# Layer 1 and the exponentials of the first four samples at other places in a planner's order

## The chip, the cores and the metric

The kernel runs on one core of a Trainium2 chip. The metric is the device time of one execution in microseconds (us). The core's engines work side by side, each through its own queue in a fixed order: TensorE (PE) for matrix products, VectorE (DVE), ScalarE (ACT), GpSimd (POOL), and SyncE (SP), which here only issues transfers. Sixteen DMA engines carry the transfers.

## What is computed

Sixteen samples of 64 x 64 tokens with 256 channels pass through four layers; each normalizes its input by groups of eight channels and adds its result. Cut to what matters:

```python
x = x + L0(_gn(x), embeddings)   # nearest of 1024 codes per token
x = x + L1(_gn(x), Wf, bf, Wg, bg, Wh, bh)
x = x + L2(_gn(x), w1, b1, w2, b2, w3, b3)
x = x + L3(_gn(x), w_qkv, w_out, b_out, gamma, beta)

# L0: indices = argmin(|x|^2 + |e|^2 - 2 x e); quantized = e[indices]
# L1: f, g, h = x Wf + bf, x Wg + bg, x Wh + bh
#     out = sigmoid(f g^T) h            (per image row of 64 tokens)
# L2: x0, x1, x2 = x.w1 + b1, x.w2 + b2, x.w3 + b3     (n = 4096 tokens)
#     sm = softmax(x0[:, :, None] * x1[:, None, :], axis=1)
#     gate = sigmoid(einsum('bn,bnm->bm', x2, sm)); out = gate * x
# L3: linear attention with 4 heads, an output projection, a layer norm
```

Layer 2 is the heavy one for DVE and ACT: for each sample 4096 x 4096 exponentials, each multiplied and summed.

## The kernel before

Each sample passes through a row of tasks, each a Python generator that emits some instructions, then yields the number of planner steps that they stand for:

- `stats0`: loads the sample in eight chunks of 512 tokens and takes the statistics of the first normalization.
- "search" (`stage1`, layer 0): 32 tiles of 128 tokens. For each, eight matmuls against the 1024 codes (L403), a DVE pass that adds and finds the largest score (L409), one that finds its index (L414), and a gather of the code's row by POOL (L415). Per chunk the result is turned round on PE (L378), its statistics are taken (L266) and it is stored.
- "layer1" (`layer1`): loads the weights, scales them by the statistics, then for eight chunks: load (L453), the projections (L482, L493), the scores (L513), their activation, and one chunk later the mixing matmuls (L533), the addition (L538), statistics (L266) and the store (L545).
- "rows" (`rows2`): reads the eight chunks again (L590), forms the three rows of layer 2 (L593), writes them to memory and reads them back spread over all partitions (`spread_rows`, L615: 1 MB for each of two rows and halves).
- "exps" (`stage2`): 64 pairs of one ACT exponential (L645, 128 x 2048) and one DVE multiply and sum (L648); at the end the gate, stored.
- "gate" (`gate2`): loads each chunk and its gates (L693, L695), ACT forms the factor (L702), DVE applies it (L703) and takes statistics, and the chunk is stored (L709).
- "layer3" (`stage3`): two passes over the chunks and the output.

Samples overlap. Times in the plan are in periods; the search of sample b has the period from b to b + 1. For every other task the planner (L946 to L958) names a time from which it may start, here `end + LAG...` after the task before it, and a length. `task` (L940) moves a start back to the end of the same kind of task of the sample before, so that exponentials of two samples never overlap in the plan, nor two layers 1. In the end a heap (L961 to L968) draws the steps of all tasks in the order of planned time: a step of s out of `total` moves its task on by `length * s / total`. The order in which the steps are drawn is the order of precedence of their instructions; the framework arranges each engine's queue by it, though an instruction that is ready may be placed before one of higher precedence that is not. Some short chains stand under `tc.high_priority` and go ahead of others.

The constants: `LAG1` 0.06 and `LEN1` 0.7 for layer 1 (0.2 long for sample 0, 0.35 for the last), `LAGR` 0.03 and 0.1 for rows, `LAG2` 0.17 from the end of layer 1 to the exponentials and 1.0 for these, `LAG3` 0.06 and `LENG` 0.8 for the gate, `LAG4` 0.04 and 1.0 for layer 3. Shorter lengths hold at the end of the batch (`LEN3`, 0.65, 0.15). The statistics of samples 1 to 7 are planned in the first 1.58 periods (`FILL`).

By this arithmetic layer 1 of samples 0, 1, 2 stands at 1.06-1.26, 2.06-2.76, 3.06-3.76; rows at 1.29-1.39, 2.79-2.89, 3.79-3.89; exponentials at 1.43-2.43, 2.93-3.93, 3.93-4.93; gates at 2.49-3.29, 3.99-4.79, 4.99-5.79; layer 3 at 3.33-4.33, 4.83-5.83, 5.83-6.83. From sample 1 on each is one period after that of the sample before.

Buffers that tie the tasks together: two wide PSUM tiles shared by L403, L493 and L533; two each of `x0b` and `x2b`, the spread rows; three of `ex`; four of `xb`, shared by the loads of stats0, rows and layer 3; three of `xm` for layer 1.

Of the kernel before, what the change touches and what calls it, by code (L numbers as in the profile page):

```python
# [32 lines left out]
LAG1, LEN1 = 0.06, 0.7  # L33
LAGR = 0.03
LAG2 = 0.17
LAG3, LENG = 0.06, 0.8
LAG4 = 0.04
LEN3 = {0: 0.4, 1: 0.33, 2: 0.37}
FILL = ((0.05, 0.95, 2), (1.0, 1.27, 3), (1.4, 1.58, 2))
EARLY = sum(n for _, _, n in FILL)  # L40


@with_exitstack
def kernel(
# [25 lines left out]
    def bank(name):  # L70
        return ps_m.tile([P, 512], F32, tag="pm", name=name)
# [60 lines left out]
    def busy(t, n):  # L132

        for _ in range(n):
            nc.tensor.matmul(
                t[:, :512], lhsT=ones3, rhs=ones3.unsqueeze(1).to_broadcast([P, 4, P]), start=True, stop=True,
                skip_group_check=True,
            )
# [174 lines left out]
    def stats0(b):  # L313
        tag = f"s0_{b}"
        st = stats_tile(0, f"st_{tag}")
        src = xT[b].rearrange("(k p) n -> p k n", p=P)
        for ch in range(NCHUNK):
            xt = xb.tile([P, NK, CW], F32, tag="xb", name=f"xs_{tag}_{ch}")
            nc.sync.dma_start(out=xt, in_=src[:, :, ch * CW : (ch + 1) * CW])
            chunk_stats(st, xt, ch)  # L320
            yield 1.5
        with tc.high_priority(offset=URGENT):
            norm0[b] = gn_finish(st, "n0", b)
        yield 2
# [242 lines left out]
    def rows2(b):  # L567
        tag = f"r2_{b}"
        scale, nmean, _ = norm2[b]
        with tc.high_priority(offset=URGENT):  # L570
            pb = bank(f"pbr_{tag}")
            busy(pb, 3)
            for k in range(NK):
                nc.scalar.activation(
                    wrow_n[:, k, :].rearrange("p (j n) -> p j n", n=32)[:, :, 0:3],
                    wrow_raw[:, k : k + 1, 0:3].to_broadcast([P, 4, 3]), AF.Copy, scale=scale[:, k : k + 1],
                )
            for k in range(NK):
                nc.tensor.matmul(
                    pb[:, 0:1], lhsT=wrow_n[:, k, :], rhs=nmean[:, k : k + 1], start=(k == 0), stop=(k == NK - 1)  # L580
                )
            brow_n = small.tile([P, 1], F32, tag="brow_n", name=f"brow_{tag}")
            nc.scalar.activation(brow_n, pb[:, 0:1], AF.Identity, bias=brow)
        x01 = small.tile([P, NT, 2], F32, tag="x01", name=f"x01_{tag}", bufs=2)
        rd = dram.tile([3, 2, 4, CW], F32, tag="rows", name=f"rows_{tag}", bufs=3)
        for h in range(2):
            pr = bank(f"pr_{tag}_{h}")
            for j in range(4):
                xt = xb.tile([P, NK, CW], F32, tag="xb", name=f"xr_{tag}_{h}_{j}")
                nc.sync.dma_start(out=xt, in_=x2_d[b][4 * h + j])  # L590
                part = slice(32 * j, 32 * j + 32)
                for k in range(NK):
                    nc.tensor.matmul(  # L593
                        pr[part, :], lhsT=wrow_n[:, k, part], rhs=xt[:, k, :], start=(k == 0), stop=(k == NK - 1)
                    )
            rows = s1p.tile([P, CW], F32, tag="t4", name=f"rows_{tag}_{h}", bufs=3)
            nc.scalar.activation(rows, pr, AF.Identity, bias=brow_n)
            for n in range(3):
                nc.scalar.dma_start(out=rd[n, h], in_=rows[n : n + 97 : 32, :])
            pt = bank(f"prt_{tag}_{h}")  # L600
            for t in range(CH):
                nc.tensor.transpose(pt[:, t * P : (t + 1) * P], rows[:, t * P : (t + 1) * P], ident)
            nc.vector.tensor_copy(
                x01[:, 16 * h : 16 * h + 16, :].rearrange("p (j t) n -> p j t n", t=CH),
                pt.rearrange("p (t j n) -> p j t n", j=4, n=32)[:, :, :, 0:2],
            )
            yield 4
        rows_d[b] = x01, rd, [spread_rows(rd, b, 0)]

    def spread_rows(rd, b, h):  # L610

        x0b = s2p.tile([P, TOK // 2], F32, tag="x0b", name=f"x0b_{b}_{h}", bufs=2)
        x2b = s2p.tile([P, TOK // 2], F32, tag="x2b", name=f"x2b_{b}_{h}", bufs=2)
        for dst, n in ((x0b, 0), (x2b, 2)):
            nc.sync.dma_start(  # L615
                out=dst, in_=rd[n : n + 1, h, :, :].rearrange("o j n -> o (j n)").to_broadcast([P, TOK // 2])
            )
        return x0b, x2b
# [314 lines left out]
    b = 0  # L933
    for begin, end, n in FILL:
        for k in range(n):
# [4 lines left out]
    def task(stage, ready, length, gen, total):  # L940
        start = max(ready, free.get(stage, 0.0))
        free[stage] = start + length
        tasks.append((start, length, gen, total))
        return start + length

    for b in range(nb):  # L946
        left = nb - 1 - b
        if b > EARLY:
            tasks.append((b - 0.7, 0.5, stats0(b), 14))
        task("search", b, 1.0, stage1(b), 160)  # L950
        end = task("layer1", b + 1 + LAG1, (LEN1 if b else 0.2) if left else 0.35, layer1(b), 88)
        task("rows", end + LAGR, 0.1, rows2(b), 8)
        if left:
            end = task("exps", end + LAG2, 1.0, stage2(b), 160)
            end = task("gate", end + LAG3, 0.15 if left == 1 else LENG, gate2(b), 36)
        else:
            end = task("exps", end + LAG2, 0.65, stage2(b, NCHUNK), 200)
        task("layer3", end + LAG4, LEN3.get(left, 1.0), stage3(b), 160)  # L958
    for _ in stats0(0):
# [45 lines left out]
```

## Time and profile before

| what | value |
|---|---|
| runs | 5691.64, 5671.38, 5691.11 us, median 5691.11 |
| profiled execution | 5674.06 us, span 5672.1 us, mean granted clock of TensorE 0.962 |
| exponentials (L648, DVE) | 1024, busy 2360.4 us, 2312 ns each |
| exponentials (L645, ACT) | 1024, busy 2138.6 us, 2089 ns each |
| score matmuls (L403, PE) | 4096, busy 1971.1 us |
| score and index (L409, L414, DVE) | busy 619.9 and 622.9 us |
| from HBM and to it | 751.18 MB and 303.04 MB, 186 GB/s over the span |

In the trace the searches (first to last L403) of samples 0 to 5 run from 31 to 175, 176 to 471, 473 to 724, 726 to 1021, 1021 to 1327 and 1334 to 1649 us; later ones take 320 to 338 us, and the last ends at 4973 us. The exponentials on ACT (L645) of samples 0 to 3 start at 322, 712, 1012 and 1309 us, and those of sample 0 end at 584. The last exponential of sample 15 starts at 5505 us.

Busy time of an engine is the union of its instructions' spans. Matmuls overlap each other in a pipeline and their ends are modelled, so a busy PE is not a PE at its peak. A view of stretches gives each engine's busy time between two moments, with the mean clock that the throttle granted to TensorE and the share of the DMA engines in use.

### The profile page before, as it was taken

The numbers are of one execution on the slowest core, as the hardware profiler recorded it, in microseconds if no ns is written. First come the engines' busy times: TensorE is split into PE (matmuls) and PEld (weight loads), VectorE is DVE, ScalarE is ACT, GpSimd is POOL, SyncE is SP. The second block draws the span as 40 slices with busy tenths as digits, with TensorE's granted clock in tenths as the row PEclk, the third lists the DMA queues.
The fourth block names the chain that finished last, engine by engine and source line by source line (L and its number), as shares of the span: only waits on it lengthen the run. The fifth ranks groups of instructions, "written<-read, shape, count | busy, mean of one in ns | idle before, by whom it ended". The sixth has DMA issues, their size and how long they took to land.

```text
span 5672.1 us, 76096 instructions
## 1 busy us (share of the span) xinstructions
PE 5162.0 (91%) x26927; PEld 3189.6 (56%) x26927; DVE 5049.3 (89%) x7186; ACT 4571.1 (81%) x6642; POOL 1801.5 (32%) x1076
## 2 busy tenths in 40 slices
PE   7977889989999999999999999999999999987788
PEld 3534446545656566565655656565565656564556
DVE  7589799899999999999999999999999999988882
ACT  4468589888989898888978888898888879887873
POOL 2223234323333333334333333333333333321221
PEclk9988999999999999999999999999999999998889
DMA  8553744655665757566575656657575675745543
GB/s 254 174 178 84 232 115 144 214 163 185 196 198 175 224 159 236 171 211 198 185 234 155 216 185 200 210 173 236 160 224 183 201 219 156 222 149 176 200 157 119
DMA packets 521365, 1059.26 MB, mean 187 GB/s; under 512 B 52504, under 2 KB 266392, under 8 KB 512792
## 3 DMA queue, kind: packets, MB, share of 16 engines
q1 hardware_dynamic: 406288, 885.11, 46.5%
q0 software_dynamic: 73728, 67.14, 8.3%
q10 hardware_dynamic: 40968, 102.13, 4.6%
q8 instruction: 214, 3.51, 0.3%
q14 instruction: 167, 1.37, 0.1%
HBM read 751.18 MB, written 303.04 MB: 186 GB/s over the span
## 4 chain that ended last, share of the span: by engine, by line
PE 46%; DVE 17%; ACT 16%; issue 6%; DMA 5%; POOL 4%; SPq 0%; ACTq 0%; DVEq 0%; POOLq 0%
PE pd_s L403 14%; ACT ex_s L645 7%; DVE ex_s L648 7%; PE ph_l L493 4%; PE pxo_s L908 3%; PE pqv_s L782 3%; PE po_l L533 2%; PE pk_s L765 2%; ACT nn_s L398 2%; POOL qv_s L802 2%; PE pz_s L857 2%; DVE i_s L414 2%; DVE nn_s L409 2%; PE pxo_s L902 2%; PE pvr_s L865 2%
## 5 line engine op out<-in xcount | busy, mean ns | idle before, releaser
L648 DVE CUSTOM_DVE_ANT_0 ex_s<-ex_s,x2b 128x2048 f32<-128x2048 f32 x1024 | 2360.4, 2312 | 77.6 <-ACT ex_s L645 74.6
L645 ACT ACTIVATE ex_s<-x0b,nmax_s,x_r 128x2048 f32<-128x2048 f32 x1024 | 2138.6, 2089 | 40.7 <-DVE num_s L648 30.5
L403 PE MATMUL pd_s<-e,xn_s 128*128 128x512 f32 x4096 | 1971.1, 614 | 43.9 <-DVE m L409 27.9
L415 POOL DMA_INDIRECT xc_s<-in_emb_rows,i_s x512 | 1113.7, 2175 | 1852.7 <-DVE i_s L414 1337.5
L403 PEld LDWEIGHTS pd_s<-e,xn_s 128*128 128x128 f32 x4096 | 745.8, 195 | 778.8 <-issue 669.1
L409 DVE CUSTOM_DVE_ANT_0 nn_s<-pd_s,nn_s 128x1024 f32<-128x1024 f32 x512 | 619.9, 1212 | 113.5 <-PE pd_s L403 63.0
L414 DVE FIND_INDEX8 i_s<-m,nn_s 128x8 uint32<-128x1024 f32 x512 | 622.9, 1217 | 0.0
L398 ACT ACTIVATE nn_s<-ne,nx_s 128x1024 f32<-128x1024 f32 x512 | 582.5, 1143 | 33.1 <-DVE nx_s L369 18.7
L493 PE MATMUL ph_l<-wh_l,xt_l 128*128 128x256 f32 x2048 | 519.6, 390 | 28.7 <-DVE m L409 16.9
L782 PE MATMUL pqv_s<-wqv_s,xk_s 128*128 128x256 f32 x2048 | 489.3, 381 | 0.0
L493 PEld LDWEIGHTS ph_l<-wh_l,xt_l 128*128 128x128 f32 x2048 | 379.7, 192 | 138.9 <-issue 69.0
L782 PEld LDWEIGHTS pqv_s<-wqv_s,xk_s 128*128 128x128 f32 x2048 | 389.1, 191 | 120.6 <-issue 59.7
L802 POOL TENSOR_TENSOR qv_s<-qv_s,qm_s 128x512 f32<-128x512 f32 x128 | 221.6, 1731 | 662.6 <-DVE qm_s L801 363.2
L868 POOL TENSOR_TENSOR lrs_s<-lrs_s,mhalf 128x4 f32<-128x4 f32 x128 | 178.0, 1391 | 677.2 <-ACT lrs_s L867 663.3
L756 POOL TENSOR_TENSOR qv_s<-qv_s,qd_s 128x512 f32<-128x512 f32 x128 | 214.4, 1675 | 249.0 <-DVE qd_s L755 132.0
L533 PE MATMUL po_l<-blk,h_l 128*128 128x128 f32 x2048 | 282.1, 288 | 3.0 <-DVE m L409 1.5
L533 PEld LDWEIGHTS po_l<-blk,h_l 128*128 128x128 f32 x2048 | 260.6, 200 | 41.1 <-issue 24.5
L908 PE MATMUL pxo_s<-wctx_s,qo_s 128*128 128x256 f32 x1024 | 269.2, 386 | 2.2 <-DVE qo_s L876 2.2
L765 PE MATMUL pk_s<-xk_s,wk_s 128*128 128x512 f32 x512 | 256.0, 620 | 1.0 <-DMA xk_s<-x_g 0.9
L913 ACT COPY y_s<-pxo_s 128x512 f32<-128x512 f32 x256 | 147.5, 580 | 132.4 <-PE pxo_s L912 116.0
L378 PE MATMUL pt_s<-ident,xc_s 128*128 128x128 f32 x1024 | 156.7, 282 | 105.2 <-DMA xc_s<-in_emb_rows,i_s 79.0
L351 ACT ACTIVATE sq_s<-xt_s,first 128x512 f32<-128x512 f32 x256 | 200.2, 806 | 37.2 <-DMA x0b<-rows_r 21.0
(206 smaller groups left out, 7322.0 us busy)
## 6 DMA issues: line engine op xcount, KB each, us to landing
xs_s<-in_xT SPq DMA_DIRECT2D x128, 512.0 KB
xt_s<-in_xT SPq DMA_DIRECT2D x128, 512.0 KB
xc_s<-in_x SPq DMA_DIRECT2D x128, 512.0 KB
x_s<-xt_s ACTq DMA_DIRECT2D x128, 512.0 KB
xt_l<-x_s SPq DMA_DIRECT2D x128, 512.0 KB
x_l<-xt_l SPq DMA_DIRECT2D x128, 512.0 KB
xr_r<-x_l SPq DMA_DIRECT2D x128, 512.0 KB
xg_g<-x_l SPq DMA_DIRECT2D x128, 512.0 KB
```

Of the source, the lines that this page charges most:

```text
L398: nc.scalar.activation(nn, ne2, AF.Identity, bias=nx2[ch][:, t : t + 1])
L403: nc.tensor.matmul(pd[:, cols], lhsT=xn[ch][:, k, t * P : (t + 1) * P], rhs=e2[:, k, cols], start=(k == 0), stop=(k == NK - 1),)
L409: nc.vector.tensor_tensor_reduce(out=nn, in0=pd, in1=nn, scale=1.0, scalar=-3.0e38, op0=ALU.add, op1=ALU.max, accum_out=m8[:, 0:1],)
L414: nc.vector.max_index(i8, m8, nn)
L415: nc.gpsimd.indirect_dma_start(out=xc[ch][:, t, :], out_offset=None, in_=emb_rows, in_offset=bass.IndirectOffsetOnAxis(ap=i8[:, 0:1], axis=0),
L493: nc.tensor.matmul(ph[:, t, :], lhsT=X[:, k, t * P : (t + 1) * P], rhs=wh_n[:, k, :], start=(t % 2 == 0 and k == 0), stop=False, skip_grou ...
L533: nc.tensor.matmul(po[:, m : m + P], lhsT=h[:, t, k * P : (k + 1) * P], rhs=at[:, t, :, :].rearrange("p r i -> p (r i)"), start=True, stop ...
L645: nc.scalar.activation(ex, x0b, AF.Exp, bias=nmax[:, T : T + 1], scale=x01[:, T, 1:2], accum_out=den[:, h, T : T + 1])
L648: nc.vector.tensor_tensor_reduce(out=ex, in0=ex, in1=x2b, scale=1.0, scalar=0.0, op0=ALU.mult, op1=ALU.add, accum_out=num[:, h, T : T + 1],)
L765: nc.tensor.matmul(pk, lhsT=wk_n[:, k, :], rhs=xt[:, k, :], start=(k == 0), stop=(k == NK - 1))
L782: nc.tensor.matmul(pqv[:, j, :], lhsT=xt[:, k, t * P : (t + 1) * P], rhs=wqv_n[:, k, :], start=(j == 0 and k == 0), stop=False, skip_group ...
L908: nc.tensor.matmul(px[:, j, :], lhsT=qT[:, t * P : (t + 1) * P], rhs=wctx[:, 1, :], start=False, stop=False, skip_group_check=True,)
```

## The change

A table `RAMP` gives samples 0 to 3 five numbers of their own: the lag of layer 1 after the search, its length, the length of rows, the lag from layer 1's end to the exponentials, and the length of these. Other samples keep the old constants.

```diff
 EARLY = sum(n for _, _, n in FILL)
+RAMP = {0: (0.03, 0.15, 0.05, 0.13, 1.25), 1: (0.04, 0.3, 0.06, 0.14, 1.2), 2: (0.05, 0.45, 0.08, 0.16, 1.14), 3: (0.06, 0.58, 0.1, 0.17, 1.08)}
...
         task("search", b, 1.0, stage1(b), 160)
-        end = task("layer1", b + 1 + LAG1, (LEN1 if b else 0.2) if left else 0.35, layer1(b), 88)
-        task("rows", end + LAGR, 0.1, rows2(b), 8)
+        early, len1, lenr, early2, lenx = RAMP.get(b, (LAG1, LEN1, 0.1, LAG2, 1.0))
+        end = task("layer1", b + 1 + early, len1 if left else 0.35, layer1(b), 88)
+        task("rows", end + LAGR, lenr, rows2(b), 8)
         if left:
-            end = task("exps", end + LAG2, 1.0, stage2(b), 160)
+            end = task("exps", end + early2, lenx, stage2(b), 160)
             end = task("gate", end + LAG3, 0.15 if left == 1 else LENG, gate2(b), 36)
```

By the same arithmetic layer 1 of samples 0 to 3 then stands at 1.03-1.18, 2.04-2.34, 3.05-3.50 and 4.06-4.64, rows at 1.21-1.26, 2.37-2.43, 3.53-3.61 and 4.67-4.77, and exponentials at 1.31-2.56, 2.56-3.76, 3.76-4.90 and 4.90-5.98. The exponentials of sample 4 start at 5.98 in place of 5.93, since those of sample 3 end there, and each later sample keeps this 0.05; gates and layer 3 follow the exponentials. Searches, the statistics ahead of them, and layer 1 and rows from sample 4 on stay where they were. No instruction and no transfer is added or taken away.

## The prediction

> **What bounds the kernel now.** I read the head of the page first, then the span cut into stretches at the places where the exponentials of a sample begin or end, then the groups of single lines. A "period" is the planner's unit: one search of a sample.
>
> ```profile
> span 5672.1 us, 76096 instructions
> PE 5162.0 (91%) x26927; PEld 3189.6 (56%) x26927; DVE 5049.3 (89%) x7186; ACT 4571.1 (81%) x6642; POOL 1801.5 (32%) x1076
> ...
> PE   7977889989999999999999999999999999987788
> ...
> DVE  7589799899999999999999999999999999988882
> ACT  4468589888989898888978888898888879887873
> ```
>
> The middle of the span is full; what is missing from VectorE (DVE) lies in the first eight slices and the last six. The DVE and ScalarE (ACT) work is the same in any order, so the sum below is made in idle DVE time. The stretches (columns: length, busy us of PE, PEld, DVE, ACT, POOL with counts, granted clock, DMA share, GB/s):
>
> ```profile
> 180.00:322.00 142.00, 135.32 (x836) 82.01 (x837) 67.95 (x117) 62.24 (x121) 23.37 (x25) 0.96 0.55 176
> 322.00:589.00 267.00, 193.23 (x778) 97.11 (x777) 254.34 (x327) 215.59 (x259) 82.70 (x39) 0.87 0.40 116
> 589.00:717.00 128.00, 113.93 (x558) 59.62 (x557) 85.61 (x149) 66.64 (x104) 29.52 (x22) 0.97 0.80 254
> 717.00:1012.00 295.00, 275.16 (x1405) 161.46 (x1404) 270.17 (x374) 259.42 (x368) 102.89 (x55) 0.96 0.46 140
> 1012.00:1309.00 297.00, 267.43 (x1392) 157.35 (x1392) 280.82 (x374) 258.94 (x352) 89.57 (x48) 0.95 0.61 191
> 1309.00:1628.00 319.00, 308.03 (x1671) 192.28 (x1670) 303.42 (x428) 283.10 (x412) 113.33 (x64) 1.00 0.62 193
> ```
>
> The first row is layer 1 of sample 0 beside the search of sample 1: PE busy 135 of 142, DVE 68. The second is exponentials of sample 0, the third the pause before those of sample 1: DVE idles 128 - 85.6 = 42.4 us. The last row is an ordinary period: 15.6 of 319 idle, 4.9%. That the third row is a pause of this kind, the line of the ACT exponentials shows, restricted to 570 to 730 us:
>
> ```profile
> L645 ACT ACTIVATE ex_s<-x0b,nmax_s,x_r x11: 2079/2088/2105, 568.4 to 729.1; 128x2048 f32<-128x2048 f32 x11
> ```
>
> Eleven in 160 us, none between 584 and 712 (the pieces of the timeline), against one every 5 us in an ordinary period (64 in 319). They are missing because sample 1's rows come last: the row matmuls (L593) run from 685 to 702, and the exponentials wait for them. And the plan's times are only an order of precedence, not a clock:
>
> ```profile
> L702 ACT ACTIVATE u_g<-gb_g,one,gn_s_n x16: 797/804/835, 604.3 to 658.4; 128x512 f32<-128x512 f32 x16
> ```
>
> These are all 16 gate activations of sample 0: planned over 0.8 of a period, they ran in 54 us of the pause. Sample 4's, in the same view, are spread over 195 us (1976 to 2171). Idle slots are already filled with later work where it is ready.
>
> **The change, part by part.** No instruction is added or removed, and no DMA or its size changes. What moves is worked out from the planner's arithmetic. Layer 1 of samples 0 to 3 goes from 1.06-1.26, 2.06-2.76, 3.06-3.76, 4.06-4.76 to 1.03-1.18, 2.04-2.34, 3.05-3.50, 4.06-4.64; exponentials from 1.43-2.43, 2.93-3.93, 3.93-4.93, 4.93-5.93 to 1.31-2.56, 2.56-3.76, 3.76-4.90, 4.90-5.98. Gates and layer 3 follow them; from sample 4 on every exponential, gate and layer 3 is 0.05 period later against searches, layer 1 and rows, which stay.
>
> (1) The pause. The exponentials of sample 1 follow those of sample 0 directly, since its rows now end at 2.43 instead of 2.89. If that stretch gets an ordinary period's idle share, DVE gains 42.4 - 0.049 x 128 = 36 us. This is the main term.
>
> (2) The earlier start of sample 0, 1.31 for 1.43. What it no longer waits for is 0.12 x 32 = 3.8 search tiles, each 8 matmuls of L403 that stood at 3.43 us in the chain of waits: 13 us. In the first row DVE idles 74 of 142, 52%; 13 us of that are 7 us. The lower bound is nothing, if the chain from layer 1's end (rows, their store, the 1 MB broadcast) sets it; I take 7.
>
> (3) The change from sample 1 to sample 2. From 717 to 1012 DVE idles 24.8 against 0.049 x 295 = 14.5 expected; the last exponential of sample 1 ends on ACT at 989, sample 2's first starts at 1012, because its row matmuls end at 999. Rows now end 0.15 period ahead of the exponentials instead of 0.04. I take 8 of the 10.3; the other two I leave to search.
>
> (4) What crowding costs. Layer 1 of sample 0 ran between 199 and 287, 88 us, beside 0.2 x 32 = 6.4 tiles of 3.43, 22 us: 66 us of PE time for layer 1. In the new 0.3 period of sample 1 PE has 66 + 9.6 tiles x 3.43 = 99 us. DVE has there 9.6 x (1.21 + 1.22) for L409 and L414, 15.4 exponentials (0.3/1.25 of 64) x 2.31, and layer 1's 8 x (1.21 + 2 x 0.68) for L538 and L266: 23 + 36 + 21 = 80. So PE sets the pace and DVE may idle 19 us. For sample 2 (0.45) the same sum is PE 66 + 49 = 115 against DVE 35 + 55 + 21 + 11 of gate = 122: nothing. For sample 3 layer 3 of sample 0 lies beside it and PE is ahead again; the nearest row is sample 1's, so 19 more at most. Bounds 0 to 38; I take 12, because sample 0's gate shows that idle slots take later work, and exponentials of the same sample are ready there.
>
> (5) The end. After the search's end (4973 us in the trace, 16.0 in the plan) 0.05 period more is left: 0.05 x 64 = 3.2 exponentials x 2.31 = 7.4 us, and 0.05/0.8 of a gate's 24 us, 1.5. As DVE work it is missing ahead of 4973, where it would have run at 95% busy; in the tail it runs at 86% (220.4 of 253 and 246.9 of 290 busy): 9/0.86 - 9/0.95 = 1 us. If the tail is set by its own chain, all 9 count. I take 5.
>
> (6) The middle, samples 4 to 13, has the same work in each period and I cost it at nothing. What hides the shift is that the change from one sample's exponentials to the next (ACT has none for 9.8 us, 2611.1 to 2620.9) is covered by search tiles. Rival B takes that cover away.
>
> (7) DMA and queues. SP's queue gets layer 1's loads and stores (16 of 512 KB per sample) in a denser order, and rows' eight loads in 0.05 to 0.1 period. From 640 to 717 the DMA share is 0.82, and layer 1 of sample 1 with its wide traffic now moves to about 500 to 589, where it is 0.35. SP's longest waits in the ramp are behind L342, for the gather (24.1 us); behind it wait only loads one or two chunks ahead. Bounds -5 to +10, taken as 0.
>
> (8) The clock. From 340 to 500 PE is busy 100.6 of 160 and its granted clock is 0.82; two more stretches without layer 1 arise (about 2.43-3.05 and 3.61-4.06). With DVE at 153.6 of 160 there, slower PE costs nothing; without that cover it is 18% of 100 us, 18 us, a bound.
> The Trainium skill's "TensorE: Matmul & The Clock Gate", section "HAM oscillation — how this bites in real kernels", speaks against the change: PE gaps over some 3.4 us drop the clock to half, so a burst after each gap starts slow. By the row the sum is left as it is; by the rule, with the 18 us paid once, it would halve to a gain of 16.
>
> Sum: -36 - 7 - 8 + 12 + 5 = -34 us. The profiled execution took 5674.06 us (span 5672.1 and 2 around it): 5640. Its runs were 5671 to 5692 with median 5691.11, 17 above the profiled one; the same 34 from the median give 5657, which I forecast.
>
> **Rivals.** A: the pause is filled and all is given back. For: the local sums of (4) reach 38, the tail 9; 36 + 7 + 8 - 38 - 9 = 4 us gained: 5687. Against: exponentials are ready during layer 1's bursts, so DVE has something to take.
>
> B, slower: the 0.05 period costs in each later period. 0.05 x 333 us (1952 to 2285) is 17 us: the change of exponentials (2611 to 2621) moves to about 2628 to 2638, right against the change of search, where PE goes from its last tile to the next sample's first (2638 to 2645; DMA share 0.97 just ahead). With neither search tiles nor exponentials DVE has only layer 3. Place: eleven changes, samples 4 to 14. Price: between nothing and the whole 9.8 us, 108 in all; I take 7.6, 84 us: 5691 - 34 + 84 = 5741. It decides from (34 + 28)/11 = 5.6 us per change. Against: the two gaps touch without overlapping, and DVE idles but 0.6 of the ten us from 2611 to 2621 now, so there is other work.
>
> C, the change doesn't do what it says: the exponentials of sample 1 wait on, since layer 1 of sample 1 is held by transfers rather than by its place. For: DMA at 0.77 and 0.82 between 589 and 717. Against: 0.35 from 500 to 589. Then only (2), (4) and (5) stand: -7 + 12 + 5, 5701.
>
> **How the numbers follow.** 0.5%, 28 us, is about what a measurement of this kernel can tell from no change. Forecast 0.47 (0.42 faster, 0.05 same), A 0.18 (same), B 0.29 (0.26 slower, 0.03 same), C 0.06 (half same, half slower): faster 0.42, same 0.29, slower 0.29. The forecast's own range runs from all gains without costs (-51) to costs at 38 with the tail at 5 (-8): 5640 to 5683; a chip that runs as the profiled one takes the lower end to 5623. To hold 8 in 10 I go to 5618, and to B's 5741 at the top; left out are B above its mean price and a little below.
>
> **What would show it.** Right: between the first samples' exponentials no gap over 25 us, DVE idle in the stretch 500 to 750 under 20 us, and the search of sample 5 ending 15 to 40 us earlier than 1975. Step 4 wrong: DVE idle over 15 us while L493 and L533 of sample 1 run. Step 6 wrong: searches of samples 7 to 13 further apart than now (327 to 338 us). Step 5 wrong: more than 710 us from the last search tile to the end (699 now).

## The result, and the profile after

| | median | lowest to highest | runs |
|---|---|---|---|
| before | 5682.09 us | 5665.41 to 5691.64 | 6 |
| after | 5730.72 us | 5727.88 to 5734.41 | 6 |

The ratio is 1.0089, with an interval of 1.007 to 1.0107: the changed kernel is slower, by 49 us, where 34 us of gain were forecast. Its profiled execution has a span of 5726.1 us, against 5672.1. The lines of the changed kernel are one higher from the planner's table on (L645 is now L646).

The head of its page, with the slices of PE and DVE:

```profile
span 5726.1 us, 76172 instructions
PE 5187.0 (91%) x26927; PEld 3214.2 (56%) x26927; DVE 5061.7 (88%) x7186; ACT 4575.6 (80%) x6642; POOL 1744.6 (30%) x1076
...
PE   7968889999999999898999989999998999987888
...
DVE  7579899998989999899999999999998999988982
```

The work is that of before: PE 5187.0 us busy for 5162.0, DVE 5061.7 for 5049.3. Of the extra 54 us of span 42 are idle time of DVE, and in 12 DVE is busy longer with the same instructions. No slice shows the idle time: DVE's fifth slice has 8 where it had 7, its third 7 where it had 8, and the middle looks as full as before. A loss of a few us in each of many periods cannot be seen in tenths. The starts of the searches (first score matmul, us) show it:

| search of sample | 2 | 3 | 4 | 5 | 6 | 7 | 8 | 9 | 14 | last one ends | span |
|---|---|---|---|---|---|---|---|---|---|---|---|
| before | 473 | 726 | 1021 | 1334 | 1656 | 1982 | 2311 | 2645 | 4322 | 4973 | 5672 |
| after | 492 | 755 | 1048 | 1354 | 1666 | 1979 | 2321 | 2663 | 4355 | 5019 | 5726 |
| later by | 19 | 29 | 27 | 20 | 10 | -3 | 10 | 18 | 33 | 46 | 54 |

At the search of sample 7 all is as it was: the changed kernel has lost 29 us and won them back. It is not the ramp that wins them all back: with the ramp alone (e1, told below) the search of sample 8 still starts 27 us late. From the search of sample 7 on the lead of the old order grows by about 5 us a period, and by 8 in the tail.

The view of stretches for the ramp of the changed kernel, up to the first exponential of sample 1 (columns: length, busy us of PE, PEld, DVE, ACT, POOL with counts, granted clock, DMA share, GB/s):

```profile
180.00:341.00 161.00, 141.50 (x830) 84.79 (x831) 68.08 (x117) 63.10 (x121) 24.27 (x24) 0.92 0.51 169
341.00:607.00 266.00, 202.82 (x934) 110.01 (x933) 252.03 (x320) 221.47 (x276) 66.08 (x35) 0.86 0.40 115
607.00:651.00 44.00, 44.00 (x209) 20.95 (x207) 27.17 (x54) 17.13 (x30) 10.22 (x10) 1.00 0.77 251
```

The third row is what is left of the pause (the last exponential of sample 0 ends at 601, the first of sample 1 starts at 651; 44 us of it from 607 on): 44 - 27.2 = 17 us of DVE idle, against 42.4 before. But the first row has grown from 142 to 161 us, with DVE busy 68 in both: 93 us idle there, against 74.

For the middle, six whole periods from search 9 to search 15, of after, of before, and of the fastest of the experiments that keep the shift (told below):

```profile
2663.50:4693.40 2029.90, 1901.73 (x10092) 1187.94 (x10092) 1891.78 (x2671) 1709.64 (x2485) 673.76 (x396) 0.98 0.62 195
```

```profile
2645.60:4656.30 2010.70, 1891.59 (x10093) 1179.24 (x10091) 1880.84 (x2668) 1705.98 (x2485) 685.24 (x397) 0.98 0.63 197
```

```profile
2637.40:4624.20 1986.80, 1877.61 (x10092) 1176.99 (x10091) 1891.60 (x2671) 1707.07 (x2483) 664.81 (x397) 0.99 0.64 200
```

After is 19.2 us longer than before. DVE idles 138.1 us in it against 129.9, 8.3 more, and is busy 10.9 longer with the same work; its multiply and sum alone takes 14.7 us more (902.3 for 887.6; the last section says beside what). So in these six periods waits make less than half of the difference between before and after. The third kernel is busy as long as after (1891.6) and idles only 95.2: between these two all of the difference is idle time.

### The profile page after: what moved, and what is told of

It reads as the page before. It is cut to its first block, busy times and chain, and to the rows that moved or that the text cites. A ratio compares the mean times of both kernels' runs of the same rounds, so it can differ in the third digit from the quotient of the medians.

```text
span 5726.1 us, 76172 instructions
## 1 busy us (share of the span) xinstructions
PE 5187.0 (91%) x26927; PEld 3214.2 (56%) x26927; DVE 5061.7 (88%) x7186; ACT 4575.6 (80%) x6642; POOL 1744.6 (30%) x1076
## 5 line engine op out<-in xcount | busy, mean ns | idle before, releaser
L649 DVE CUSTOM_DVE_ANT_0 ex_s<-ex_s,x2b 128x2048 f32<-128x2048 f32 x1024 | 2376.3, 2330 | 68.4 <-ACT ex_s L646 67.5
L646 ACT ACTIVATE ex_s<-x0b,nmax_s,x_r 128x2048 f32<-128x2048 f32 x1024 | 2139.6, 2090 | 45.6 <-DVE num_s L649 42.0
L404 PE MATMUL pd_s<-e,xn_s 128*128 128x512 f32 x4096 | 1966.6, 616 | 74.4 <-DVE m L410 37.1
L416 POOL DMA_INDIRECT xc_s<-in_emb_rows,i_s x512 | 1061.5, 2073 | 2059.1 <-DVE i_s L415 1209.3
L404 PEld LDWEIGHTS pd_s<-e,xn_s 128*128 128x128 f32 x4096 | 756.3, 196 | 843.3 <-issue 708.4
L410 DVE CUSTOM_DVE_ANT_0 nn_s<-pd_s,nn_s 128x1024 f32<-128x1024 f32 x512 | 620.4, 1214 | 122.5 <-PE pd_s L404 88.4
L869 POOL TENSOR_TENSOR lrs_s<-lrs_s,mhalf 128x4 f32<-128x4 f32 x128 | 201.7, 1575 | 543.6 <-ACT lrs_s L868 543.6
L766 PE MATMUL pk_s<-xk_s,wk_s 128*128 128x512 f32 x512 | 284.2, 677 | 0.0
L757 POOL TENSOR_TENSOR qv_s<-qv_s,qd_s 128x512 f32<-128x512 f32 x128 | 183.1, 1431 | 322.3 <-DVE qd_s L756 226.5
L534 PEld LDWEIGHTS po_l<-blk,h_l 128*128 128x128 f32 x2048 | 247.5, 192 | 42.2 <-issue 30.8
L534 PE MATMUL po_l<-blk,h_l 128*128 128x128 f32 x2048 | 261.3, 278 | 1.7 <-DVE m L410 0.8
L349 ACT ACTIVATE xn_s<-xt_s,first 128x512 f32<-128x512 f32 x256 | 202.2, 806 | 58.5 <-PE pd_s L404 28.2
```

The source lines that it names most:

```text
L404: nc.tensor.matmul(pd[:, cols], lhsT=xn[ch][:, k, t * P : (t + 1) * P], rhs=e2[:, k, cols], start=(k == 0), stop=(k == NK - 1),)
L410: nc.vector.tensor_tensor_reduce(out=nn, in0=pd, in1=nn, scale=1.0, scalar=-3.0e38, op0=ALU.add, op1=ALU.max, accum_out=m8[:, 0:1],)
L416: nc.gpsimd.indirect_dma_start(out=xc[ch][:, t, :], out_offset=None, in_=emb_rows, in_offset=bass.IndirectOffsetOnAxis(ap=i8[:, 0:1], axis=0),
L534: nc.tensor.matmul(po[:, m : m + P], lhsT=h[:, t, k * P : (k + 1) * P], rhs=at[:, t, :, :].rearrange("p r i -> p (r i)"), start=True, stop ...
L646: nc.scalar.activation(ex, x0b, AF.Exp, bias=nmax[:, T : T + 1], scale=x01[:, T, 1:2], accum_out=den[:, h, T : T + 1])
L649: nc.vector.tensor_tensor_reduce(out=ex, in0=ex, in1=x2b, scale=1.0, scalar=0.0, op0=ALU.mult, op1=ALU.add, accum_out=num[:, h, T : T + 1],)
```

## The experiments

Two things were in the change: a new ramp (samples 0 to 3), and a shift of 0.05 period of exponentials, gates and layer 3 against searches, layer 1 and rows of every later sample, which comes only from the last number of the table. The first theory was that the shift is the loss; the rival, that the crowded ramp is.

**Ramp and shift apart.** `e1_ramp_no_shift` keeps the ramp and takes back the 0.05:

```diff
-... 3: (0.06, 0.58, 0.1, 0.17, 1.08)}
+... 3: (0.06, 0.58, 0.1, 0.17, 1.03)}
```

> The changed kernel with one number changed: the exponentials of sample 3 take 1.03 periods instead of 1.08, so that from sample 4 on every task has its old place and only the first periods differ from the kernel before. Theory S (the shift of 0.05 period costs about 4.8 us in each of some ten later periods): searches of samples 7 to 13 again 328 to 338 us apart, time 5670 to 5690 by the profiled execution, 0.99 to 1.00 of before. Theory R (the crowded first periods cost it): the 50 us stay, 5720 to 5735.

Measured: 1.0019 [1.0, 1.0037], 5693 us. `e2_shift_only` is the kernel before with the 0.05 alone:

```diff
-            end = task("exps", end + LAG2, 1.0, stage2(b), 160)
+            end = task("exps", end + LAG2, 1.05 if b == 3 else 1.0, stage2(b), 160)
```

> The kernel before with one number changed: the exponentials of sample 3 take 1.05 periods, so that exponentials, gates and layer 3 from sample 4 on come 0.05 later, and nothing else moves. Theory S: 45 to 55 us slower than before, searches of samples 7 to 13 some 5 us further apart each, ACT's pause between two samples' exponentials 15 to 18 us instead of 10. Theory R: within 10 us of before.

Measured: 1.0083 [1.0061, 1.0104], 5725 us. The shift alone is the loss, and the ramp alone is worth nothing. In the trace of e2 the loss begins late: its search of sample 7 starts 10 us before that of the kernel before, its search of sample 15 32 us after it, and its span is 50 us longer. `e8_ramp_old_sample0` is e1 with sample 0 at its old lags, so that only samples 1 to 3 are crowded:

```diff
-RAMP = {0: (0.03, 0.15, 0.05, 0.13, 1.25), ... 3: (..., 1.08)}
+RAMP = {0: (0.06, 0.2, 0.1, 0.17, 1.13), ... 3: (..., 1.03)}
```

> The changed kernel without the shift, and with the old numbers of sample 0 (layer 1 at 1.06 to 1.26, rows 0.1, exponentials from 1.43, 1.13 long so that they still end at 2.56). If the denser layer 1 and rows of sample 0 cost the 19 us by which its exponentials began later in the changed kernel (341 for 322): first exponential at 322, 15 to 20 us faster than the ramp without the shift, 0.998 to 1.000 of before. If the loss lies in samples 1 to 3: 1.001 to 1.003 as without it.

Measured: 1.0001 [0.9981, 1.0021], 5682 us. The first exponential comes at 325 us again, and DVE's idle time in the search of sample 1 is 81 us (before 83, after 101, e1 98). So the delay of sample 0 is undone, but the total hardly moves: in the five periods from search 1 to search 6 DVE idles 191 us before, 209 after, 207 in e1 and 201 in e8.

**Which part of the shift.** `e3_exps_only_late` delays only the exponentials, and lets gate and layer 3 keep their places:

```diff
+            end = task("exps", end + LAG2, 1.05 if b == 3 else 1.0, stage2(b), 160)
+            end = task("gate", end + (LAG3 if b < 3 else LAG3 - 0.05), ...)
```

> As the run with the shift alone, but gates from sample 3 on start 0.05 period sooner after the exponentials, so that gates and layer 3 have their old places and the exponentials alone are late. If the change of exponentials against the change of search is the place of the loss (S1): 35 to 50 us slower than before, ACT's pause 15 to 18 us. If gates and layer 3 are (S2): under 15 us slower.

Measured: 1.009 [1.0063, 1.0117], 5737 us. `e4_gate_layer3_late` does the reverse:

```diff
+            end = task("gate", end + (LAG3 if b < 3 else LAG3 + 0.05), ...)
```

> The kernel before with gates and layer 3 from sample 3 on 0.05 period later and the exponentials at their old places. S1: under 15 us slower than before, ACT's pause near 10 us. S2: 35 to 50 us slower. Both in part if the two losses add up.

Measured: 1.0061 [1.0041, 1.0082], 5712 us. Each alone costs about as much as both together, so the loss is no sum over the tasks moved. (The profiled run of e4 is its fastest, 5699.5 us. Of its 26 us over before only 5 lie in the six periods from search 8 to search 14.) The next question was how it goes with the distance. `e5_shift_015` and `e6_shift_0025` are e2 with 1.15 and 1.025 for 1.05.

> The kernel before with a shift three times as large: the exponentials of sample 3 take 1.15 periods, so exponentials, gates and layer 3 from sample 4 on come 0.15 later. Theory K (the change of exponentials must not stand at the change of search): 0.15 carries it past the change of search, so the period is again near 335 us and only the end is longer, by some 10 to 25 us: 1.002 to 1.005 of before. Theory L (each further delay costs in proportion): three times the 47 us of the shift by 0.05, 1.02 to 1.025 of before.

> The kernel before with half the shift: the exponentials of sample 3 take 1.025 periods. In the plan their change then ends before the last tile of the search. Theory K: under 12 us slower than before. Theory L: 20 to 27 us slower.

Measured: 1.0364 [1.0336, 1.0392], 5882 us, and 1.0073 [1.0045, 1.0101], 5717 us. Half the shift costs as much as the whole one, and three times the shift more than four times as much: neither of the two theories expected holds, and there is no proportion near zero.

**The order of the queues at the change of exponentials.** PE's longest waits in those six periods, by group (engine, line, who ended the wait: us in total, times, longest), for after and then before:

```profile
PE pg_n L286 <- DVE mv_n L282: 30.2, 6, 5.0
PE pd_s L404 <- DVE gate_s L657: 26.3, 6, 5.0
```

```profile
PE px_s L357 <- ACT sq_s L351: 15.9, 19, 1.8
PE prt_r L602 <- ACT rows_r L597: 12.4, 6, 2.6
```

Two waits, of 5.0 us (L286) and 4.4 us (L404) on the mean, stand in each of the six periods of after; before has no group with one over 2.7. During the first DVE has work without a pause (3020.6 to 3026 in the period shown next), so it costs DVE nothing there. The timeline of PE in after shows the second, at the end of the exponentials of sample 7:

```profile
2992.26 1.04 PE L379 MATMUL pt_s<-ident,xc_s 128*128 128x128 f32 x8
2993.13 3.60 PE L404 MATMUL pd_s<-e,xn_s 128*128 128x512 f32 x8
3000.71 6.65 PE L404 MATMUL pd_s<-e,xn_s 128*128 128x512 f32 x8 [3.98 <-DVE gate_s L657]
3007.19 0.27 PE L667 MATMUL pgt_s<-ident,gate_s 128*32 128x128 f32 x1
3007.30 1.88 PE L766 MATMUL pk_s<-xk_s,wk_s 128*128 128x512 f32 x4
```

From 2996.73 to 3000.71 PE does nothing, and the next eight score matmuls take 6.65 us instead of 3.60. They are the first of the search of sample 10: the wait stands at the change of search, inside the pause between the exponentials of samples 7 and 8 (2992.5 to 3008.9). In before the search changes later, at 2973 to 2979, with the exponentials of the next sample under way since 2955.9, and PE has layer 3's matmuls there and no wait. The eight matmuls wait for a wide PSUM tile that DVE frees by reading it. DVE in the same stretch:

```profile
2995.93 1.29 DVE L267 BATCH_NORM_STATS2 st_s<-xt_s 128x6 f32<-128x512 f32 x2 [2.21 <-ACT xt_s L382]
2997.14 2.27 DVE L649 CUSTOM_DVE_ANT_0 ex_s<-ex_s,x2b 128x2048 f32<-128x2048 f32 x1
...
2999.34 1.22 DVE L410 CUSTOM_DVE_ANT_0 nn_s<-pd_s,nn_s 128x1024 f32<-128x1024 f32 x1
...
3000.48 0.19 DVE L657 TENSOR_TENSOR gate_s<-den_s 128x32 f32<-128x32 f32 x1
```

The reading is L410, at 2999.34 (L657, which the profile names, is the instruction that ends last before the matmuls). It stands behind L267, which waited 2.21 us, and one more exponential. L267 waits for ACT, and ACT for POOL:

```profile
2994.80 0.63 ACT L804 ACTIVATE qv_s<-qv_s 128x512 f32<-128x512 f32 x1 [2.25 <-POOL qv_s L803]
2995.33 1.05 ACT L382 COPY xt_s<-pt_s 128x512 f32<-128x512 f32 x2
...
3002.90 0.23 ACT L662 ACTIVATE gate_s<-gate_s 128x32 f32<-128x32 f32 x1 [1.61 <-DVE gate_s L661]
3007.50 0.26 ACT L669 COPY grow_s<-pgt_s 32x128 f32<-32x128 f32 x1 [4.38 <-PE pgt_s L667]
```

Behind PE's score tile stand the gate's transposition (L667), whose input was ready at 3004.5, and layer 3's projections (L766), which need nothing of the gate. So ACT waits 4.38 us for the copy of the gate row (L669), in front of the first exponential of sample 8, at 3008.88. In before the row was copied (L668) after one exponential of the next sample and without a wait:

```profile
2955.92 2.09 ACT L645 ACTIVATE ex_s<-x0b,nmax_s,x_r 128x2048 f32<-128x2048 f32 x1 [0.93 <-DVE nmax_s L632]
...
2959.17 0.24 ACT L668 COPY grow_s<-pgt_s 32x128 f32<-32x128 f32 x1
```

At the changes from sample 7 to sample 14 this wait of ACT is 1.9 to 4.5 us in after. In e3, e4 and f1 (told below), which lose as well, it is nothing at all of these changes but one (2.2 us, e3).

`e7_shift_row_later` keeps the whole shift of e2 and moves the transposition, the copy of the row and what follows by 7 of the 160 steps of the task, 0.04 period:

```diff
             nc.vector.reciprocal(gate, gate)
-            yield 1
+            yield 8 if parts == 1 else 1
             pg = bank(f"pgt_{tag}_{part}")
```

> The shift by 0.05 alone, and in the exponentials' last steps the transposition of the finished gates and its copy on ACT come 7 steps (0.044 period) later, behind the first exponentials of the next sample. If ACT's wait for that transposition (3.9 us per change, with DVE idle 2.7 behind it) is a main part of the loss: 20 to 35 us faster than the shift alone, 1.002 to 1.005 of before. If it is not: 1.008 as with the shift alone.

Measured: 0.9968 [0.9953, 0.9984], 5661 us: with the shift, and faster than before and after. Its waits on PE are short again:

```profile
PE pxt_s L364 <- ACT xrow_s L362: 19.4, 18, 2.3
PE prt_r L602 <- ACT rows_r L597: 16.3, 6, 2.7
```

And its timeline of PE at the same place shows that the wait for POOL is still there, but with other work in front of the score tile:

```profile
2956.82 1.04 PE L378 MATMUL pt_s<-ident,xc_s 128*128 128x128 f32 x8
2957.70 1.88 PE L765 MATMUL pk_s<-xk_s,wk_s 128*128 128x512 f32 x4
2961.81 1.99 PE L782 MATMUL pqv_s<-wqv_s,xk_s 128*128 128x256 f32 x8 [2.23 <-ACT xt_s L381]
...
2965.80 4.46 PE L403 MATMUL pd_s<-e,xn_s 128*128 128x512 f32 x10
```

ACT waits 3.54 us for POOL there and DVE 3.39 for ACT, more than in after. But layer 3's matmuls (L765, L782) run meanwhile, PE's gap is 2.23 us, and the next ten score matmuls take 4.46 us, at the rate of the eight in 3.60. The change of search (2969) lies inside the pause (2957.0 to 2973.6) here too, and PE has no wait in front of the next search's first tile. The pause between the exponentials of two samples on ACT is 14 to 17 us, as in after (15 to 17) and e2 (14 to 19), against 10 in before: its length is not what costs.

How much of it lies at this place? The sums of six stretches of 40 us, each from 10 us before the end of a sample's exponentials to 30 us after it (samples 7 to 12), for before, after and e7:

```profile
sum 240.00, PE 221.48 PEld 126.10 DVE 209.38 ACT 188.12 POOL 87.28; mean PE 36.91 PEld 21.02 DVE 34.90 ACT 31.35 POOL 14.55
sum 240.00, PE 197.40 PEld 106.64 DVE 192.10 ACT 184.93 POOL 76.49; mean PE 32.90 PEld 17.77 DVE 32.02 ACT 30.82 POOL 12.75
sum 240.00, PE 212.53 PEld 118.16 DVE 208.23 ACT 175.44 POOL 85.33; mean PE 35.42 PEld 19.69 DVE 34.70 ACT 29.24 POOL 14.22
```

DVE idles 5.1 us at a change in before, 8.0 in after and 5.3 in e7. So the change holds all that after idles more than before (2.5 us a period, in the table below). But of the 8 us of idle time a period that e7 has less than after, only 2.7 lie here. The rest comes from elsewhere in the period, and was not traced.

`e11_shift_copy_later` was to separate the copy from the transposition: e2 with 7 steps between them.

```diff
             nc.tensor.transpose(pg[:n, :P], gate, ident)
+            if parts == 1:
+                yield 7
             grow = small.tile([NT, P], F32, tag="grow", ...)
```

> The shift by 0.05 alone, with the transposition on PE at its old place and only its copy on ACT 7 steps later (its PSUM bank, one of four, is then held some 14 us longer). If ACT's queue standing still behind the copy makes the loss: near the mended shift, 0.996 to 1.001 of before. If the place of the transposition in PE's queue makes it, or the bank is missed: 1.005 to 1.010.

Measured: 1.0066 [1.0047, 1.0086], 5718 us. But its trace has the copy at the old place in ACT's queue (from sample 6 to 13 in front of all of the next exponentials, with a wait of 1.9 to 4.4 us), so it tells little beyond this: without moving the transposition the loss stays. `e9_changed_row_later` puts the edit of e7 into the changed kernel, `e10_before_row_later` into the kernel before, `e12_ramp_row_later` into e1.

> The changed kernel as it is, ramp and shift, with the transposition of the finished gates and its copy on ACT 7 steps later, as in the run that mended the shift alone. If the whole loss of the changed kernel was that row in front of the next exponentials: 0.995 to 1.000 of before. If the ramp and the shift add something that this does not mend: 1.003 to 1.008.

Measured: 0.9976 [0.9958, 0.9994], 5667 us: the edit takes off the whole loss of the changed kernel and a little more.

> The kernel before, no ramp and no shift, with the same row 7 steps later. There the row stands behind one exponential already. If the gain of the mended shift over before (0.9968) comes from the row's place alone: 0.994 to 0.999 here too. If it needs the shift: 0.999 to 1.003.

Measured: 1.0121 [1.0085, 1.0156], 5746 us.

> The changed kernel without the shift (exponentials of sample 3 1.03 long), with the row 7 steps later. If the ramp itself is worth nothing: equal to the kernel before with the row later, within 0.2%. If the pause that it shortens is worth something once the changes of sample run smoothly: 0.002 to 0.006 below that.

Measured: 1.0113 [1.0072, 1.0154], 5742 us. So the edit isn't good in itself: it gains 1.1% on the shifted order and loses 1.2% on the unshifted one, which neither expectation had. That it puts the row back to where, in a shifted plan, it fits, is a reading; it is also one more displacement.

**How small a displacement is enough.** `f1_shift_001` and `f2_shift_008` are e2 with 1.01 and 1.08.

> The kernel before with a shift by 0.01 period (exponentials of sample 3 1.01 long). If the loss grows with the place (0.025: 1.0073, 0.05: 1.0083, 0.15: 1.0364): 1.000 to 1.004. If it depends on the order that the framework happens to make: anything from 0.995 to 1.010, also below 1.

> The kernel before with a shift by 0.08. If the loss grows with the place: 1.010 to 1.020, between the shifts by 0.05 and 0.15. If it depends on the order: it may be below 1.008, and the sum of PE's gaps of over 2 us per period tells which (2.5 us before, 13 with the shift by 0.05).

Measured: 1.0148 [1.0129, 1.0168], 5769 us, and 1.0164 [1.0147, 1.0181], 5778 us. Over 0.01, 0.025, 0.05, 0.08 and 0.15 the loss is 1.5, 0.7, 0.8, 1.6 and 3.6%: a fifth of the shift costs nearly twice as much as all of it. Nor is a distance in the plan a distance in time: from the end of sample 7's exponentials to the first score matmul of search 10 there are 33 us in before, 16 with the shift by 0.01 (3 us in the plan) and 9 with that by 0.05. `g1_layer3_001` and `g2_layer1_001` move another task by 0.01 period:

```diff
-LAG4 = 0.04
+LAG4 = 0.05
...
-LAG1, LEN1 = 0.06, 0.7
+LAG1, LEN1 = 0.07, 0.69
```

> The kernel before with layer 3 starting 0.01 period later after the gate (LAG4 0.05), exponentials and all else in their places. If the kernel before stands at a favourable order in general: 1.005 to 1.015. If only the exponentials' place matters: 0.998 to 1.003.

> The kernel before with layer 1 of all samples but the last starting 0.01 period later and ending at the same place (LAG1 0.07, LEN1 0.69), exponentials in their places (sample 0's, which follow its layer 1, come 0.01 later). If the kernel before stands at a favourable order in general: 1.005 to 1.015. If only the exponentials' place matters: 0.998 to 1.003.

Measured: 1.0076 [1.0054, 1.0097], 5727 us, and 1.0038 [1.0024, 1.0052], 5701 us. It needs no shift of exponentials at all. In g1 the loss lies in the first periods (search 6 starts at 1689 us, before at 1656) and the later periods are even shorter than before's.

**POOL's subtraction.** The chain above starts at POOL (L802, the subtraction of the largest query in layer 3's softmax). Without it and the maximum (L800 to L802), in e2 and in the kernel before, the shift should cost nothing if it starts there:

```diff
-            qm = small.tile([P, CH, HEADS], F32, tag="qm", ...)
-            nc.vector.tensor_reduce(qm, q4, AX.X, ALU.max)
-            nc.gpsimd.tensor_tensor(q4, q4, qm....to_broadcast(...), ALU.subtract)
```

> The shift by 0.05, with the finding and subtracting of each head's largest query in layer 3 left out (the same softmax without its guard; one DVE and one POOL instruction less per chunk, 128 each). If ACT's standing behind that POOL instruction starts the loss: the difference to the next kernel, which has no shift, falls from 0.8% to under 0.3%, and PE's gaps of over 2 us fall from 13 to under 6 us per period. If not: the difference stays at 0.5 to 1%.

> The kernel before, with the same two instructions of layer 3 left out: the measure for the kernel above. 128 DVE reductions of 0.68 us are 87 us of DVE work less; where DVE sets the pace, 0.985 to 0.99 of before, under either theory.

Measured: 0.9844 [0.9828, 0.986], 5592 us, and 0.9762 [0.9746, 0.9778], 5546 us. Between the two the shift still costs 0.83% (5592 / 5546 = 1.0083), as with the subtraction. PE's wait in front of the next search's first tile is down to some 1.2 us in the first of them (4 to 7 in e2), and yet DVE idles 8.5 us at a change of exponentials, against 4.9 without the shift. That theory fell: the wait for this subtraction is one link in the chain of one order, and without it the shift costs as much. The kernel before gained more than the 1 to 1.5% expected from DVE's 87 us: it also idles less, 14.6 us a period for 21.7.

All of these beside each other, as means over the six periods from search 8 to search 14, with the longest wait among PE's four costliest groups of waits:

| kernel | ratio | period, us | DVE idle, us | PE's longest wait, us |
|---|---|---|---|---|
| before | 1 | 335.2 | 21.7 | 2.6 |
| after | 1.0089 | 339.1 | 24.2 | 5.0 |
| e1 ramp | 1.0019 | 334.6 | 20.7 | 2.6 |
| e8 ramp, old sample 0 | 1.0001 | 334.2 | 20.7 | 3.5 |
| e2 shift 0.05 | 1.0083 | 339.6 | 24.8 | 7.3 |
| e11 shift, copy later | 1.0066 | 339.1 | 24.2 | 5.0 |
| e3 exponentials only | 1.009 | 340.4 | 26.0 | 3.7 |
| e4 gate, layer 3 only | 1.0061 | 336.0 | 19.9 | 3.3 |
| f1 shift 0.01 | 1.0148 | 341.9 | 29.2 | 5.3 |
| e6 shift 0.025 | 1.0073 | 339.8 | 23.8 | 7.1 |
| f2 shift 0.08 | 1.0164 | 345.3 | 30.6 | 8.0 |
| e5 shift 0.15 | 1.0364 | 353.4 | 37.8 | 12.1 |
| g1 layer 3 by 0.01 | 1.0076 | 332.5 | 21.8 | 6.2 |
| g2 layer 1 by 0.01 | 1.0038 | 340.8 | 24.5 | 3.4 |
| e10 before, row later | 1.0121 | 337.8 | 23.2 | 2.6 |
| e12 ramp, row later | 1.0113 | 338.2 | 23.5 | 3.3 |
| e7 shift, row later | 0.9968 | 331.1 | 16.0 | 2.7 |
| e9 changed, row later | 0.9976 | 331.4 | 16.1 | 2.7 |

Period less DVE idle is 311 to 316 us in every row: DVE's work is what fills a period, and in most rows the larger part of a period's loss or gain is what DVE idles in it (not in e4, e6 and g1). Where PE's longest wait is 5 us and over the period is longer, but for g1; the reverse does not hold (e3, g2, e10, e12). So the wait traced above stands where after and e2 lose, and is not a law for the others. That it is the price even there is a reading: taking it away took the loss away in e7 and e9, and left it without POOL's subtraction.

## Why the prediction was wrong, step by step

**The step that failed is (6).** "The middle, samples 4 to 13, has the same work in each period and I cost it at nothing. What hides the shift is that the change ... is covered by search tiles." The work is the same; its order on the queues isn't. Searches 8 to 14 stand 339.1 us apart instead of 335.2, and e2, which has this shift alone, has the whole loss (1.0083). The cover that step (6) named is what failed in the trace of after: at the change of exponentials the next search's first tile stood ahead of layer 3's matmuls in PE's queue, with its PSUM tile not yet free, and held them up, and DVE idles 8.0 us at a change for 5.1. In e7 it stood behind them. That search tiles are there as work says nothing of whether they are ready at the head of the queue.

**(1) The pause**: in part. DVE's idle time during the search of sample 2 fell from 49 to 31 us, 18 of the 36 forecast; from 500 to 750 us it was 31 us, above the 20 named beforehand. Layer 1 of sample 1 ran from 521 to 615, its row matmuls until 641, and the exponentials began 50 us after those of sample 0 ended: above the 25 named beforehand. The forecast put an ordinary period's idle share in place of the pause; what set the start is still the chain of layer 1, rows and exponentials.

**(2) The earlier start of sample 0**: wrong sign. Its rows did end earlier (last row matmul 307.9 us, before 312.0), but the first exponential started at 341 instead of 322. The timeline of ACT in after shows what stood in front of it:

```profile
325.08 1.07 ACT L382 COPY xt_s<-pt_s 128x512 f32<-128x512 f32 x2 [7.28 <-PE pt_s L379]
...
335.31 0.27 ACT L363 COPY xrow_s<-px_s 128x128 f32<-128x128 f32 x1 [4.79 <-PE px_s L358]
337.84 3.23 ACT L399 ACTIVATE nn_s<-ne,nx_s 128x1024 f32<-128x1024 f32 x3 [2.26 <-DVE nx_s L370]
340.97 2.08 ACT L646 ACTIVATE ex_s<-x0b,nmax_s,x_r 128x2048 f32<-128x2048 f32 x1
```

And in before:

```profile
320.26 2.17 ACT L398 ACTIVATE nn_s<-ne,nx_s 128x1024 f32<-128x1024 f32 x2
322.33 2.08 ACT L645 ACTIVATE ex_s<-x0b,nmax_s,x_r 128x2048 f32<-128x2048 f32 x1
...
330.89 1.07 ACT L381 COPY xt_s<-pt_s 128x512 f32<-128x512 f32 x2 [6.39 <-PE pt_s L378]
```

In before the exponential was placed ahead of the copy L381, which then waited 6.39 us for PE. In after this copy and two more instructions of the search of sample 1 are ahead of it, and wait 7.28 + 4.79 + 2.26 = 14.3 us, while no wait is recorded of the exponential itself; the longest goes back to a gather, on which PE waits:

```profile
324.57 0.90 PE L379 MATMUL pt_s<-ident,xc_s 128*128 128x128 f32 x3 [6.90 <-DMA xc_s<-in_emb_rows,i_s]
```

The start was costed by the tiles that it no longer waits for; the tiles that came to be in front of it in ACT's queue were not counted. Its lower bound was nothing, and the loss is 18 us of DVE idle in that search (83 to 101). e8, with the old lags of sample 0, has it back (81).

**(3) The change from sample 1 to 2** gave 5 us of idle time instead of 8 (25 to 20), and the searches of samples 4 and 5 lose 22 (16.4 to 22.6, 18.2 to 34.1), which no step had. **(4) The crowding** was put at 12: while layer 1 of sample 1 runs (521 to 615) DVE idles 94 - 86.6 = 7 us, under the 15 named, with PE busy 91 of 94, as the sum said. The cost of the ramp is thus not in the burst but behind it, and why DVE idles more during searches 4 and 5 was not tried. Summed, (1) to (4) gave +18 us of idle time, not -39, and e1 puts the ramp alone at 1.0019. For the ramp rival A had the outcome, that all is given back; its reason, the local sums of (4), is not what the trace shows.

**(5) The end**: +8 us from the end of the last search (699.1 to 707.1), forecast 5, bound 9. Under the 710 named.

**(7) DMA and queues**: the order of SP's queue did no harm that the runs show. Both halves of sample 0's `x0b` were asked for earlier than before (305.3 and 314.7 us, against 307.0 and 318.5). **(8) The clock** was costed at nothing, and in six periods it went from 0.982 to 0.976 of full, 0.993 in e7. Small, but of the kind weighed there: after PE's gap of 3.98 us eight matmuls took 6.65 us, with a granted clock of 0.55, where eight others took 3.60 with 1.00. The Trainium skill's "TensorE: Matmul & The Clock Gate", section "HAM oscillation — how this bites in real kernels", says that gaps past some 3.4 us drop the clock to half, and this row agrees with it. The gaps that the rule warned of came not in the ramp but in each later period.

**Rival B** had the place right (the later periods, at the change of exponentials) and the total near (5741; 5731 measured). What it saw is in the trace of after: the change of search (2996.7 to 3000.7) inside the change of exponentials (2992.5 to 3008.9). Its price was too high and its count too: 7.6 us a change at eleven changes, where the period grew by 4 to 5 us, and only from the search of sample 7 on. And the meeting of the two changes is not enough for the loss: e7 has it too, with the longer pause, and is the fastest. The price also should have grown with the distance, and 0.01 costs more than 0.05.

One line of the tests named beforehand was misnumbered: the search that ends at 1975 us is that of sample 6. It ended at 1978.

**What stays open.** Why the order before is so good, which queue position starts the loss in e3, e4, g2, e10 and e12, and where in the period e7 gains most of what it gains, is not settled. Of ten displaced versions of the kernel before (e2 to e6, f1, f2, g1, g2 and e10) all lose, by 0.4 to 3.6%; e7, displaced twice, gains 0.3%. That it stands at a favourable point of a rugged surface, rather than that each displacement has a cause of its own kind, is a reading of that list and not shown.

## What to carry to other kernels

Where queues keep a fixed order and a plan decides it, a change at the front that displaces everything behind it has to be priced by the period times the number of periods: here some 5 us in each of the eight periods from the search of sample 7 to that of sample 15, and 17 us from there to the end, outweighed any gain in a ramp that occurs once. Try the displacement alone, with one number, before reading anything into the part that was meant to gain. And look, for each engine, at what is at the head of its queue and not ready: a busy share, or work that exists, does not cover a wait that stands in front of it.

## What the runs showed of the hardware

**DVE beside POOL.** DVE's multiply and sum takes 2.28 us, but up to 4.5 beside POOL's element-wise operations on SBUF. A stretch of the timeline in after:

```profile
3815.89 1.55 POOL L416 DMA_INDIRECT xc_s<-in_emb_rows,i_s  x1 [9.08 <-DVE qd_s L756]
...
3816.23 4.45 DVE L649 CUSTOM_DVE_ANT_0 ex_s<-ex_s,x2b 128x2048 f32<-128x2048 f32 x1
...
3816.89 1.64 POOL L757 TENSOR_TENSOR qv_s<-qv_s,qd_s 128x512 f32<-128x512 f32 x1
...
3820.74 2.27 DVE L649 CUSTOM_DVE_ANT_0 ex_s<-ex_s,x2b 128x2048 f32<-128x2048 f32 x1
```

4.45 us, with a gather's issue (1.55) and a scaling (1.64) of POOL inside, and 2.27 for the next one. In after 46 of 1024 are over 2.5 us, 52 us in excess; in before 38 and 35 us, and this is most of why their mean went from 2312 to 2330 ns. All of these long ones have an element-wise operation of POOL inside; of the 312 in after that overlap the issue of a gather alone none is over 2.5 us. And 44 of the 46 end 2.15 us after POOL's operation does, nearly the whole time that one takes undisturbed, as here (3818.53 and 3820.68), though another 210 that overlap such an operation are not over 2.5 us. The Trainium skill's "SBUF — State Buffer", section "SBUF: two separate sides", has a lock between a GpSimd operation that reads SBUF and a DVE instruction with two inputs there, under which one waits for the whole of the other's instruction; the long ones agree with it. The excess doesn't set the order of the kernels: e7 has 66 such, 54 us, and is the fastest with the shift.

**Gaps in POOL's queue.** Before a subtraction (L802) POOL stands for some 8 us with nothing that the profile shows as its releaser, here in e2:

```profile
2975.60 2.89 POOL L415 DMA_INDIRECT xc_s<-in_emb_rows,i_s  x1 [0.69 <-issue]
2986.48 1.04 POOL L802 TENSOR_TENSOR qv_s<-qv_s,qm_s 128x512 f32<-128x512 f32 x1 [7.99 <-issue]
```

The timeline leaves out what POOL's sequencer does there: at 2977.95 it has a pair of `MODIFY_POOL_CONFIG`. Such pairs stand on both sides of each sample's reduction over all partitions (L629, at the start of a sample's exponentials), here as the kernel before has them:

```profile
L629 POOLq MODIFY_POOL_CONFIG  x32: 8/632/657, 309.1 to 5215.2; - x32
L629 POOL PARTITION_ALL_REDUCE ab_s<-ext_s x16: 372/373/1868, 316.7 to 5220.9; - x16
```

In before, after and e2 each has 32 pairs, one in front of each reduction and one in front of the operation that follows it, and from each pair to the next operation 5.6 to 11 us pass. That the pair is what takes them is a reading of these 32 places. In e2 the gap is the first link of the chain shown above, and it comes with the exponentials, which the shift moves. No run leaves the reduction out, so whether the shift would cost less without these gaps is open. Without the subtraction and its maximum the order before takes 2.4% less.
